# The output of the selective scan: three chunks of tokens in rotation instead of two

## The chip, the cores and the metric

The kernel runs on one core of a Trainium2 chip. The metric is the time of one execution on the device in microseconds (us), lower is better. Three runs of the kernel before the change took 13265.99, 13266.81 and 13270.98 us; the median is 13266.81. A profiled execution is a separate run, with its own time.

A core has several engines that work side by side, each through its own instructions in order: TensorE (PE, matrix products; PEld is its loading of weights), VectorE (DVE), ScalarE (ACT) and GpSimd (POOL). SyncE (SP) issues data transfers. They wait for one another through semaphores. SBUF is the on-chip memory with 128 partitions, PSUM the memory with eight banks into which PE writes.

## The reference, cut to what matters

The network takes four images of 56 x 56 positions with 128 channels. Each image passes four layers, each of the form x = x + layer(group_norm(x)): window attention, a selective state-space scan (mamba), a deformable convolution, and window attention again. The change touches only the end of the second layer, behind the scan:

```python
# y: sum of the four scan directions, 256 channels; z: second half of group_norm(x) @ w_in
mu = jnp.mean(y, axis=-1, keepdims=True)
var = jnp.mean(jnp.square(y - mu), axis=-1, keepdims=True)
y = (y - mu) * jax.lax.rsqrt(var + LN_EPS) * ln_w + ln_b
y = y * jax.nn.silu(z)
return y @ w_out
...
x = x + _L1_conv_ref(_gn(x), ...)
```

So each position needs a layer norm over 256 channels, a gate silu(z), a product with w_out (256 to 128 channels) and a residual addition. Channels lie on the partitions, in two halves of 128, so the mean and the variance over channels are matrix products.

## The kernel before

`run` (L1368) works through the images one after the other: `swin("L0")`, `mamba`, `deform`, `swin("L3")`. `mamba` calls `mamba_conv`, `mamba_scan` and `mamba_out` in turn; the change is in `mamba_out` (L1139 to L1198), which runs once per image, four times in all. The result of the scan lies in `ya` (two halves, 3136 positions), the residual stream in `x`.

`mamba_out` cuts the 3136 positions of an image into NCK = 7 chunks of CH = 448. The pool is opened under `manual_schedule()`: the instructions of each engine stay in the order in which the program writes them, so the order of the calls is the schedule. All its PSUM tiles share one tag with eight banks, taken in rotation. These are the steps for a chunk c:

- `mean`: PE multiplies `ya` by a matrix that yields minus the mean (`pm`, two products, L1149). DVE adds `pm` to each half of `ya` and gets the centred `xc` (L1153); ACT squares both halves into `sq` (L1155).
- `gate`: DVE normalizes the chunk of `x` with the group norm's mean and deviation into `xg` (`gn_apply`, L137). For each half, PE multiplies by `w_in` (`pz`, L1163) and ACT applies Silu into `z` (L1164).
- `spread`: PE sums the squares (`ln_pv`, L156, eight small products), ACT takes the square root (L158), DVE the reciprocal (L159), giving `ln_rs`, with positions on the partitions.
- `scale`: PE turns `ln_rs` and spreads it over all partitions (`ln_pb`, L1173, four products); DVE multiplies each half of `xc` by it (L1175), ACT applies `ln_w` and `ln_b` (Identity with scale and bias, L1177), DVE multiplies by `z` (L1178).
- `out`: PE multiplies `xc` by `w_out` (`pmo`, L1184), DVE adds the result to `x` (L1185) and takes the statistics for the next group norm (`stats`, L115).

An fp32 product appears in the profile as more than one matmul record: `pm`, `pz` of both halves and `pmo` have four each, `ln_pb` eight, `ln_pv` sixteen. ACT needs a table load (ACT_TABLE_LOAD) when it goes from Silu to Sqrt or back.

The order of the calls is a loop over the chunks at L1188 to L1198: `spread(c)`, `mean(c+1)`, `gate(c+1)`, `out(c-1)`, `scale(c)`. Behind the stage, `deform` (L1213) starts with a memset of `gp` on POOL (L1229) and with a group norm that needs the statistics of all seven chunks.

Of the kernel before, what the change touches and what calls it, by code (L numbers as in the profile page):

```python
# [10 lines left out]
F32 = mybir.dt.float32  # L11
# [8 lines left out]
P = 128  # L20
HW = 56
L = HW * HW
CH = 448
NCK = L // CH
# [54 lines left out]
class _Net:  # L79
# [1057 lines left out]
            assert not plan and not soon  # L1137

    def mamba_out(self, x, ya, gn):  # L1139
        nc, tc, w = self.nc, self.tc, self.w["L1"]  # L1140
        with tc.tile_pool(name="mo", bufs=2) as sb, tc.tile_pool(name="mo_ps", bufs=8, space=PSUM) as ps, tc.manual_schedule():
            bank = lambda name: ps.tile([P, 512], F32, tag="mm", name=name)
            part = lambda c: slice(c * CH, (c + 1) * CH)
            m = {}

            def mean(c):
                pm = bank("pm")
                for j in range(2):
                    nc.tensor.matmul(pm[:, :CH], lhsT=self.center[2][1], rhs=ya[:, j, part(c)], start=(j == 0), stop=(j == 1))  # L1149
                xc = m["xc", c] = sb.tile([P, 2, CH], F32, tag="xc", name="xc", bufs=3)  # L1150
                sq = m["sq", c] = sb.tile([P, 2, CH], F32, tag="sq", name="sq")
                for j in range(2):
                    nc.vector.tensor_add(xc[:, j, :], pm[:, :CH], ya[:, j, part(c)])  # L1153
                for j in range(2):
                    nc.scalar.activation(sq[:, j, :], xc[:, j, :], AF.Square)  # L1155

            def gate(c):
                xg = sb.tile([P, CH], F32, tag="xg", name="xg2")
                self.gn_apply(xg, x[:, part(c)], gn)
                z = m["z", c] = sb.tile([P, 2, CH], F32, tag="z", name="z", bufs=3)  # L1160
                for j in range(2):
                    pz = bank("pz")
                    nc.tensor.matmul(pz[:, :CH], lhsT=w["w_in"][:, (2 + j) * P : (3 + j) * P], rhs=xg, start=True, stop=True)  # L1163
                    nc.scalar.activation(z[:, j, :], pz[:, :CH], AF.Silu)  # L1164

            def spread(c):
                m["rs", c] = self.ln_spread(m.pop(("sq", c)), bank, sb)

            def scale(c):
                xc, rs = m["xc", c], m.pop(("rs", c))  # L1170
                pb = bank("ln_pb")
                for i in range(CH // QB):
                    nc.tensor.matmul(pb[:, i * QB : (i + 1) * QB], lhsT=rs[:, i : i + 1].to_broadcast([QB, P]), rhs=self.ident[:QB, :QB], start=True, stop=True)  # L1173
                for j in range(2):
                    nc.vector.tensor_mul(xc[:, j, :], pb[:, :CH], xc[:, j, :])  # L1175
                for j in range(2):
                    nc.scalar.activation(xc[:, j, :], xc[:, j, :], AF.Identity, bias=w["ln_b"][:, j : j + 1], scale=w["ln_w"][:, j : j + 1])  # L1177
                nc.vector.tensor_mul(xc, xc, m.pop(("z", c)))  # L1178

            def out(c):  # L1180
                xc = m.pop(("xc", c))
                po = bank("pmo")
                for j in range(2):
                    nc.tensor.matmul(po[:, :CH], lhsT=w["w_out"][:, j * P : (j + 1) * P], rhs=xc[:, j, :], start=(j == 0), stop=(j == 1))  # L1184
                nc.vector.tensor_add(x[:, part(c)], x[:, part(c)], po[:, :CH])  # L1185
                self.stats(x, c)

            mean(0)  # L1188
            gate(0)
            for c in range(NCK):  # L1190
                spread(c)
                if c + 1 < NCK:
                    mean(c + 1)
                    gate(c + 1)
                if c >= 1:
                    out(c - 1)
                scale(c)
            out(NCK - 1)  # L1198


    def deform_prepare(self):
# [269 lines left out]
```

## Time and profile before

| what | value |
|---|---|
| median of three runs | 13266.81 us |
| the profiled execution | 13274.82 us |
| its span, first to last instruction | 13273.0 us |
| PE busy | 11709.4 us (88%) |
| POOL busy | 9942.5 us (75%) |
| DVE busy | 9579.6 us (72%) |
| ACT busy | 7564.2 us (57%) |
| mean granted PE clock | 0.933 of full |
| group L1153, DVE, two additions per chunk | 56 x, median 615 ns |
| group L1155, ACT, two squares per chunk | 56 x, median 576 ns |
| group L1164, ACT, two Silu per chunk | 56 x, median 543 ns |
| group L1164, ACT, table load | 28 x, 1283 ns |
| group L1175, DVE, two products per chunk | 56 x, median 614 ns |
| group L1177, ACT, two scalings per chunk | 56 x, median 754 ns |
| group L1178, DVE, product with z | 28 x, median 1093 ns |
| group L1185, DVE, addition to x | 28 x, median 622 ns |

28 is seven chunks in four images. The profile gives each instruction's start and length. In a timeline, neighbouring instructions of one kind are merged into a row with their count; a bracket at the end gives how long the engine stood idle before the row and which instruction, by engine, tile and line, ended the wait. "issue" there means that the profile shows nothing that it waited for. Two instructions of one engine can overlap a little[...]. The ends of matmuls are modelled. The granted clock is the share of PE's full speed that it was allowed.

### The profile page before, as it was taken

The numbers are of one execution on the slowest core, as the hardware profiler recorded it, in microseconds if no ns is written. First come the engines' busy times: TensorE is split into PE (matmuls) and PEld (weight loads), VectorE is DVE, ScalarE is ACT, GpSimd is POOL, SyncE is SP. The second block draws the span as 40 slices with busy tenths as digits, with TensorE's granted clock in tenths as the row PEclk, the third lists the DMA queues.
The fourth block names the chain that finished last, engine by engine and source line by source line (L and its number), as shares of the span: only waits on it lengthen the run. The fifth ranks groups of instructions, "written<-read, shape, count | busy, mean of one in ns | idle before, by whom it ended". The sixth has DMA issues, their size and how long they took to land. (4 is left out here: it accounts for less than half of the span.)

```text
span 13273.0 us, 218239 instructions
## 1 busy us (share of the span) xinstructions
PE 11709.4 (88%) x85716; PEld 7457.0 (56%) x85716; DVE 9579.6 (72%) x11831; ACT 7564.2 (57%) x19130; POOL 9942.5 (75%) x6852
## 2 busy tenths in 40 slices
PE   8999995799999999579999899956998989995799
PEld 4448883444544888344454488834445448883444
DVE  6649996665564999666566599966646649996664
ACT  5567772356556777235655677723565567772356
POOL 4949994488494999448849499944975949994497
PEclk9999997799999999779999999977999999997799
DMA  2000004200000000420000000042000000004200
GB/s 100 1 14 4 5 4 116 79 1 7 5 1 14 4 5 4 115 80 1 7 5 1 14 4 5 4 118 77 1 8 4 1 14 5 5 4 123 71 1 6
DMA packets 181178, 344.60 MB, mean 26 GB/s; under 512 B 20104, under 2 KB 101416, under 8 KB 180024
## 3 DMA queue, kind: packets, MB, share of 16 engines
q0 software_dynamic: 80640, 231.28, 6.2%
q1 hardware_dynamic: 99224, 97.83, 2.3%
q8 instruction: 678, 11.11, 0.3%
q14 instruction: 348, 2.85, 0.1%
q10 hardware_dynamic: 288, 1.53, 0.0%
HBM read 256.04 MB, written 74.52 MB: 25 GB/s over the span
## 5 line engine op out<-in xcount | busy, mean ns | idle before, releaser
L555 POOL TENSOR_TENSOR es<-es,e 128x896 f32<-128x896 f32 x2016 | 4159.6, 2088 | 132.6 <-ACT e L549 74.7
L350 DVE TENSOR_REDUCE mx<-pm 128x1 f32<-128x512 f32 (+1 forms) x4928 | 3059.2, 672 | 1404.8 <-PE pm L349 790.7
L549 ACT ACTIVATE e<-pst 128x448 f32<-128x448 f32 (+1 forms) x5600 | 2677.8, 544 | 1893.5 <-PE pst L547 1349.3
L1066 DVE TENSOR_TENSOR_SCAN hs<-da,dbu 128x928 f32<-128x928 f32 x1792 | 3633.5, 2071 | 54.3 <-ACT dbu L1059 29.0
L1075 POOL TENSOR_TENSOR hs<-hs,cb 128x896 f32<-128x896 f32 x1792 | 3484.2, 1961 | 26.9 <-ACT carry L1070 21.9
L349 PE MATMUL pm<-ks,qs 32*128 32x512 f32 (+1 forms) x9856 | 2912.8, 636 | 13.3 <-DVE nm L371 7.8
L547 PE MATMUL pst<-qs,ks 32*128 32x448 f32 x11200 | 2685.8, 548 | 0.0
L1084 PE MATMUL yt<-w_C,hs 128*116 128x128 f32 x14336 | 1866.1, 273 | 1.1 <-POOL hs L1075 1.1
L542 PE MATMUL pst<-nm,sel 32*128 32x448 f32 x5600 | 1639.2, 614 | 0.0
L1084 PEld LDWEIGHTS yt<-w_C,hs 128*116 128x116 f32 x14336 | 1570.8, 135 | 2.1 <-POOL hs L1075 2.1
L1048 PE MATMUL dbu<-dgb,ut 112*128 112x224 f32 x7168 | 1258.4, 298 | 268.9 <-DVE hs L1066 268.8
L571 PE MATMUL po<-e,va 128*32 128x448 f32 (+1 forms) x11200 | 1352.4, 551 | 0.1
L349 PEld LDWEIGHTS pm<-ks,qs 32*128 32x128 f32 x9856 | 925.9, 186 | 744.0 <-DVE mx L350 617.8
L1308 POOL DMA_INDIRECT g<-tab,idx x1008 | 940.3, 933 | 453.5 <-issue 429.7
L1048 PEld LDWEIGHTS dbu<-dgb,ut 112*128 112x128 f32 x7168 | 945.4, 192 | 534.4 <-DVE hs L1066 524.4
L1002 ACT ACTIVATE da<-dl,A 128x112 f32<-128x112 f32 x3584 | 1194.5, 383 | 0.1
L547 PEld LDWEIGHTS pst<-qs,ks 32*128 32x128 f32 x11200 | 1098.7, 185 | 102.3 <-issue 13.7
L1334 PE MATMUL pvt<-w_C,g 112*128 112x112 f32 x2016 | 400.1, 365 | 735.6 <-issue 610.6
L542 PEld LDWEIGHTS pst<-nm,sel 32*128 32x128 f32 x5600 | 571.0, 184 | 739.9 <-DVE mx L350 387.1
L1335 ACT COPY vt<-pvt 128x336 f32<-128x336 f32 x336 | 147.2, 438 | 1190.6 <-PE pvt L1334 1186.1
L1334 PEld LDWEIGHTS pvt<-w_C,g 112*128 112x128 f32 x2016 | 312.7, 201 | 827.4 <-issue 791.1
L1070 ACT COPY carry<-hs 128x32 f32<-128x32 f32 x1792 | 397.8, 222 | 624.4 <-DVE hs L1066 616.1
(230 smaller groups left out, 15785.8 us busy)
## 6 DMA issues: line engine op xcount, KB each, us to landing
tab<-zero SPq DMA_DIRECT2D x4, 6728.0 KB
g<-tab,idx POOLq DMA_INDIRECT x1008, 3.4
tab<-gt SPq DMA_DIRECT2D x32, 448.0 KB
dl_d<-dl SPq DMA_DIRECT2D x28, 448.0 KB
dl<-dl_d SPq DMA_DIRECT2D x56, 224.0 KB
tab<-gt SPq DMA_DIRECT2D x32, 336.0 KB
out_dram<-x SPq DMA_DIRECT2D x28, 224.0 KB
x<-in_x_dram SPq DMA_DIRECT2D x21, 224.0 KB
```

Of the source, the lines that this page charges most:

```text
L349: nc.tensor.matmul(pm[:, :m], lhsT=qs[head(h), q.start : q.start + P], rhs=ks[head(h), keys], start=True, stop=True)
L350: nc.vector.tensor_reduce(mx[:, home[i][1], h, kc : kc + 1], pm[:, :m], AX.X, ALU.max)
L542: nc.tensor.matmul(t[:, :CH], lhsT=self.sel[head(h), :], rhs=nm[head(h), part(qc)], start=True, stop=False)
L547: nc.tensor.matmul(t[:, :CH], lhsT=ks[head(h), k * KB : (k + 1) * KB], rhs=qs[head(h), part(qc)], start=False, stop=True)
L549: nc.scalar.activation(e[:nk, j, :], t[:nk, :CH], AF.Exp, scale=SCALE)
L555: nc.gpsimd.tensor_tensor(s, es[g - 1, p][:nk] if k == 1 else s, e[:nk], ALU.add)
L571: nc.tensor.matmul(m["po"][head(h), :CH], lhsT=va[:nk, k, head(h)], rhs=src(h)[:nk], start=(k == 0), stop=(k == NKB - 1))
L1002: nc.scalar.activation(m["da"][:, :, n, 2:], dl(), AF.Exp, scale=A[:, j, n : n + 1])
L1048: nc.tensor.matmul(pu[:, 8 * h : 8 * h + 8, 2 + tb * TB : 2 + (tb + 1) * TB], lhsT=made[g]["ut", 2 * r + tb][:, d, :], rhs=made["r", g // ...
L1066: nc.vector.tensor_tensor_scan(flat(pairs[u // 2][:, d % 2]), flat(made[g]["da"][:, r]), flat(banks.pop(u)), 0.0, ALU.mult, ALU.add)
L1075: nc.gpsimd.tensor_tensor(hs, hs, made["r", g // 2]["cb"][:, :, r * HW : (r + 1) * HW], ALU.mult)
L1084: nc.tensor.matmul(sums[q][:YR, e * P : (e + 1) * P], lhsT=hs[:, n, :], rhs=self.ident, start=(n == 0), stop=(n == NST // 2 - 1), is_trans ...
```

## The change

The steps are cut finer and put into a new order. `mean` keeps only the product on PE; `less` takes the additions and squares. `tokens` takes the normalization out of `gate`. `gated` takes the product with z out of `scale`. `out` keeps only the product, and `store` takes the addition to `x` and the statistics. The loop runs over c from -1 to NCK and calls, where the chunk exists: `mean(c+1)`, `gated(c-1)`, `less(c+1)`, `scale(c)`, `gate(c+1)`, `out(c-1)`, `tokens(c+2)`, `spread(c+1)`, `store(c-1)`. So the chunks c-1, c and c+1 are at work in one round, and `xg` is made one round before its use. The tile `xc` has four buffers in place of three. The instructions themselves, their shapes and their number stay as they are.

```diff
--- before.py
+++ after.py
@@ -1137,6 +1137,8 @@
             assert not plan and not soon
 
     def mamba_out(self, x, ya, gn):
+
+
         nc, tc, w = self.nc, self.tc, self.w["L1"]
         with tc.tile_pool(name="mo", bufs=2) as sb, tc.tile_pool(name="mo_ps", bufs=8, space=PSUM) as ps, tc.manual_schedule():
             bank = lambda name: ps.tile([P, 512], F32, tag="mm", name=name)
@@ -1144,19 +1146,25 @@
             m = {}
 
             def mean(c):
-                pm = bank("pm")
+                pm = m["pm", c] = bank("pm")
                 for j in range(2):
                     nc.tensor.matmul(pm[:, :CH], lhsT=self.center[2][1], rhs=ya[:, j, part(c)], start=(j == 0), stop=(j == 1))
-                xc = m["xc", c] = sb.tile([P, 2, CH], F32, tag="xc", name="xc", bufs=3)
+
+            def less(c):
+                pm = m.pop(("pm", c))
+                xc = m["xc", c] = sb.tile([P, 2, CH], F32, tag="xc", name="xc", bufs=4)
                 sq = m["sq", c] = sb.tile([P, 2, CH], F32, tag="sq", name="sq")
                 for j in range(2):
                     nc.vector.tensor_add(xc[:, j, :], pm[:, :CH], ya[:, j, part(c)])
                 for j in range(2):
                     nc.scalar.activation(sq[:, j, :], xc[:, j, :], AF.Square)
 
+            def tokens(c):
+                m["xg", c] = sb.tile([P, CH], F32, tag="xg", name="xg2")
+                self.gn_apply(m["xg", c], x[:, part(c)], gn)
+
             def gate(c):
-                xg = sb.tile([P, CH], F32, tag="xg", name="xg2")
-                self.gn_apply(xg, x[:, part(c)], gn)
+                xg = m.pop(("xg", c))
                 z = m["z", c] = sb.tile([P, 2, CH], F32, tag="z", name="z", bufs=3)
                 for j in range(2):
                     pz = bank("pz")
@@ -1175,27 +1183,36 @@
                     nc.vector.tensor_mul(xc[:, j, :], pb[:, :CH], xc[:, j, :])
                 for j in range(2):
                     nc.scalar.activation(xc[:, j, :], xc[:, j, :], AF.Identity, bias=w["ln_b"][:, j : j + 1], scale=w["ln_w"][:, j : j + 1])
+
+            def gated(c):
+                xc = m["xc", c]
                 nc.vector.tensor_mul(xc, xc, m.pop(("z", c)))
 
             def out(c):
                 xc = m.pop(("xc", c))
-                po = bank("pmo")
+                po = m["po", c] = bank("pmo")
                 for j in range(2):
                     nc.tensor.matmul(po[:, :CH], lhsT=w["w_out"][:, j * P : (j + 1) * P], rhs=xc[:, j, :], start=(j == 0), stop=(j == 1))
-                nc.vector.tensor_add(x[:, part(c)], x[:, part(c)], po[:, :CH])
+
+            def store(c):
+                nc.vector.tensor_add(x[:, part(c)], x[:, part(c)], m.pop(("po", c))[:, :CH])
                 self.stats(x, c)
 
-            mean(0)
-            gate(0)
-            for c in range(NCK):
-                spread(c)
-                if c + 1 < NCK:
-                    mean(c + 1)
-                    gate(c + 1)
-                if c >= 1:
-                    out(c - 1)
-                scale(c)
-            out(NCK - 1)
+            def do(f, c):
+                if 0 <= c < NCK:
+                    f(c)
+
+            tokens(0)
+            for c in range(-1, NCK + 1):
+                do(mean, c + 1)
+                do(gated, c - 1)
+                do(less, c + 1)
+                do(scale, c)
+                do(gate, c + 1)
+                do(out, c - 1)
+                do(tokens, c + 2)
+                do(spread, c + 1)
+                do(store, c - 1)
 
 
     def deform_prepare(self):
```

## The prediction

> **What bounds the kernel now.** The page's own tables don't show this stage: its groups are too small for the costliest list and its lines are not in the chain of waits. I therefore asked the tiles that the change touches for their times, then the busy time of the stage in each of the four images. It runs from the first `pm` matmul behind the scan to the end of the last `stats` on `x`; columns are window, length, then busy time (count) of PE, weight loads, DVE, ACT, POOL, then the granted PE clock and the DMA share.
>
> ```profile
> core 0: us, PE busy (x) PEld busy (x) DVE busy (x) ACT busy (x) POOL busy (x), PEclk, DMA share, GB/s
> 2029.18:2110.27 81.09, 57.54 (x252) 35.49 (x252) 35.70 (x63) 44.21 (x63) 1.26 (x1) 0.92 0.00 1
> 5347.31:5429.53 82.22, 58.37 (x252) 35.38 (x252) 35.59 (x63) 44.31 (x63) 1.26 (x1) 0.88 0.00 0
> 8661.98:8745.21 83.23, 59.67 (x252) 36.12 (x252) 35.70 (x63) 44.32 (x63) 1.26 (x1) 0.86 0.00 0
> 11969.03:12052.10 83.07, 59.35 (x252) 36.16 (x252) 35.72 (x64) 44.31 (x63) 1.26 (x1) 0.86 0.00 1
> ```
>
> The stage takes 329.6 us of 13273.0 (2.5%). Nothing else runs beside it (POOL 1.26, no DMA), and no engine is full: PE 71%, ACT 54%, DVE 43%. The next stage starts from its last `stats`, so a microsecond saved here is one off the end. The limit must be a loop of waits between engines; the timeline of one round without a slow clock (2062.08 to 2072.01, 9.93 us: PE 7.21 busy, ACT 6.27, DVE 5.04) shows it, engine by engine. First DVE, then ACT, then PE:
>
> ```profile
> 2062.28 0.62 DVE L1185 TENSOR_TENSOR x<-x,pmo 128x448 f32<-128x448 f32 x1 [3.43 <-PE pmo L1184]
> 2062.94 0.63 DVE L115 BATCH_NORM_STATS2 gn_st<-x 128x6 f32<-128x448 f32 x1
> 2063.48 1.14 DVE L1175 TENSOR_TENSOR xc<-ln_pb,xc 128x448 f32<-128x448 f32 x2
> 2065.57 1.09 DVE L1178 TENSOR_TENSOR xc<-xc,z 128x896 f32<-128x896 f32 x1 [0.95 <-ACT xc L1177]
> 2067.14 0.18 DVE L159 RECIPROCAL ln_rs<-ln_rs 112x4 f32<-112x4 f32 x1 [0.48 <-ACT ln_rs L158]
> 2067.24 1.13 DVE L1153 TENSOR_TENSOR xc<-pm,ya 128x448 f32<-128x448 f32 x2
> 2068.28 0.51 DVE L137 TENSOR_SCALAR xg<-x,gn_mean,gn_rstd 128x448 f32<-128x448 f32 x1
> ```
> ```profile
> 2064.12 1.41 ACT L1177 ACTIVATE xc<-xc,w_L 128x448 f32<-128x448 f32 x2 [2.79 <-DVE xc L1175]
> 2065.55 1.28 ACT L158 ACT_TABLE_LOAD   x1
> 2066.85 0.26 ACT L158 ACTIVATE ln_rs<-ln_pv,eps 112x4 f32<-112x4 f32 x1
> 2067.93 1.04 ACT L1155 ACTIVATE sq<-xc 128x448 f32<-128x448 f32 x2 [0.82 <-DVE xc L1153]
> 2068.99 1.28 ACT L1164 ACT_TABLE_LOAD   x1
> 2070.29 0.98 ACT L1164 ACTIVATE z<-pz 128x448 f32<-128x448 f32 x2
> ```
> ```profile
> 2068.93 1.74 PE L1163 MATMUL pz<-xg,w_L 128*128 128x448 f32 x4 [2.72 <-DVE xg L137]
> 2070.51 1.67 PE L1184 MATMUL pmo<-xc,w_L 128*128 128x448 f32 x4
> 2072.01 1.04 PE L1173 MATMUL ln_pb<-w_C,ln_rs 112*128 112x112 f32 x8
> 2072.89 1.65 PE L156 MATMUL ln_pv<-w_C,sq 128*112 128x1 f32 x16
> 2074.40 1.75 PE L1149 MATMUL pm<-ya,w_C 128*128 128x448 f32 x4
> 2078.86 3.18 PE L1163 MATMUL pz<-xg,w_L 128*128 128x448 f32 x4 [2.71 <-DVE xg L137]
> ```
>
> The reader is to see one ring. DVE's store (2062.28), stats and two products feed ACT's scaling (2064.12); behind that stand the table load and the square root (2066.85); the reciprocal, two additions and `xg` follow on DVE; `xg` frees PE's `pz` (2068.93), and `pmo` follows, for which the next store waits (3.43 us). In the ring PE stands idle 2.7 us a round. The last PE row is the same `pz` at a slow clock, 3.18 for 1.74; such rounds took 11.3 to 11.4 us instead of 9.93, so the slow clock lies on the path. From the throttle-free pieces I put a stage together: first `pm` to first `ln_pb` 11.7 (image 1), next round 11.27 less 1.5, four rounds of 9.93, last round 6.2, drain about 8: 75.4. The four stages have a mean of 82.4, so the slow clock costs about 7.0 each.
>
> **What the Trainium skill says.** Perfetto Trace Analysis, Per-engine timelines: ACT and DVE are strict FIFO; the trace agrees, every row above is in program order. ScalarE: Activation LUTs, What ACT_TABLE_LOAD costs: 1283 ns and a drain of 1380 ns. The trace agrees on the first (1283 in every one), not on the second: sqrt starts 0.02 after its load, and the load 0.02 after the scaling. I use 1.285. Same page, Table sets: cheap functions such as identity are in every set; the trace shows Identity (L1271) behind the group norm's Sqrt, and Square (L1155) behind L158, without a load. TensorE: Matmul & The Clock Gate, Part 1: a PE idle for about 3.4 us falls to half clock. Here 2.7 us sufficed now and then, and 3.4 us always (the last `pmo` took 3.3 in all four images).
>
> **The change part by part.** No instruction is added or removed; `xc` gets a fourth buffer. The order per round becomes: PE `pm`(c+1), `ln_pb`(c), `pz`(c+1), `pmo`(c-1), `ln_pv`(c+1); DVE product with z (c-1), two additions (c+1), two products (c), `xg`(c+2), reciprocal (c+1), store and stats (c-1); ACT two squares (c+1), two scalings (c), load, two Silu (c+1), load, sqrt (c+1). Table loads stay two a round, since Silu and Sqrt still alternate.
>
> *Waits that go.* `pz` finds `xg` made a round ago, `pmo` its product, the store its `pmo`. *Wait that is late next.* The reciprocal stands on DVE ahead of store, stats, product with z and additions, although none of them needs it; ACT reaches its sqrt only behind both loads, and its next squares wait for these additions. So a new ring of ACT and DVE. Lags from the rows above (start to start): sqrt to reciprocal 0.29, reciprocal 0.10, store 0.65, stats 0.54, product with z 1.0 (1.09 less the overlap of neighbours), addition to square 0.66, squares 1.07, scalings 1.40, load 1.285, Silu 0.98, load 1.285: 9.26 us a round. `ln_pb` and the products on it end 0.1 us before ACT asks for them. PE needs 6.9 of 9.26 and waits 2.36 at `ln_pb`, for the reciprocal.
>
> *PE's slack.* A half clock adds at most about 1.5 us to a round's PE work, as above. `ln_pb` has 1.0 us before DVE comes to it (and loses 0.9), `pz` 3.3, `pmo` over 5, `ln_pv` 2.4, `pm` 3. So I cost the slow clock at nothing in the middle; if the cover were gone, it is 1.5 in each such round, as today.
>
> *Buffers.* Six banks a round of eight: each bank is reused by an instruction whose predecessor in it was read a round earlier. `sq`, `xg`, `ln_rs` with two, `z` with three, `xc` with four also find theirs free. Cost nothing. The memset of `gp` on POOL behind the stage still has the group norm's 6.5 us as cover.
>
> *The sum for one stage.* First `pm` to first sqrt: 1.72 + 0.66 + 1.07 + 1.285 + 0.98 + 1.285 = 7.0. To the second: 7.25 (no store, no product with z; the scaling waits for `ln_pb`). To the third: 9.26 less store and stats = 8.07. Four full rounds: 37.04. Drain behind the last sqrt: 0.29 + 0.10 + 1.19 + 1.24 to `pmo`(5), 1.71 to its store, 1.19, product with z 1.24, `pmo`(6) 1.71, store and stats 1.3: 9.97. Sum 69.3. Laid out in the same way the old order gives 74.1 against 75.4 above, so the way is short by about 1.2: 70.5. Slow clock: the first `pm` in three of four images, +0.8 each, so 0.6 in the mean; both `pmo` in the drain, +1.5 each (waits of 1.4 and 2.6 us on PE behind one of 3.9). 74.1 per stage against 82.4: 8.3 saved, times 4 is 33 us. The profiled execution took 13274.8 (span 13273.0 and 1.8 around it), 8 above the median of 13266.8; so 13241 for such an execution and 13233 for the median.
>
> **Bounds.** No slow clock at all and no shortfall: 69.3, saves 52. As much slow clock as today (7.0 on 70.5): saves 4.9 a stage, 20. What a measurement of this kernel can tell from no change is about 0.2%, 26.5 us.
>
> **Rivals.**
> 1. *The new ring is hardly shorter* and slow clock remains: 9.26 against 9.93 is only 0.67 a round; if PE's waits at `ln_pb` bring as many slow windows and these reach DVE (`ln_pb` has just 0.1 us to spare at half clock), 20 us: 13247. For it: the 2.36 us of idle PE in every round. Against: everything but `ln_pb` has over 2 us of slack.
> 2. *PE becomes the bound* at about 7.3 a round, if ACT and DVE overlapped better than in my order: 5 rounds shorter by 2 more, 4 times: 40 more, 13193. Against: ACT alone has 6.27 a round, and between sqrt and squares it stands idle 3 us.
> 3. *Slower: PE stays at half clock through whole rounds.* Then its 6.9 is 13.8, above the ring. Fully cold stages: 7 x 4 x (13.8 - 9.3) = 126 on top of -33, 13360. From 27% of cold rounds on the change loses. For it: PE is now idle once in every round. Against: the gap is shorter than today's 2.7, which left most rounds fast.
> 4. *Slower: further table loads*, if Identity behind Sqrt called for one and Silu for another: 2 x 1.285 x 28 = 72, 13306. Against: L1271.
>
> **How the numbers follow.** Forecast (saving over 26.5, around 33) 0.74; rival 1 0.14; rival 2 0.04; rivals 3 and 4 0.08. Faster 0.78, same 0.14, slower 0.08. Range from the bounds, reaching a little past both: 13212 to 13254.
>
> **What shows each step.** Right: a middle round of 9.2 to 9.5 us in all images, slow clock or not; DVE's longest wait at the reciprocal for ACT's sqrt (4 us a round), PE's at `ln_pb` for the reciprocal, ACT's at the squares (3 us); no wait for `xg` or at the store but in the drain; 14 loads a stage; stages of 72 to 76. Wrong: rounds over 9.9 or under 9, waits at `pm` or `pz` for banks, a third load, or stretches at half clock through whole rounds.

## The result and the profile after

The changed kernel takes 13235.55 us in the median of 10 runs (13223.56 to 13245.72); the kernel before, on the same chips, 13269.67 (13261.48 to 13305.55). The ratio, worked out from the single runs and so not the quotient of the two medians (0.9974), is 0.997 with a 95% interval of 0.9961 to 0.998; the medians lie 34 us apart. The span of the profiled execution went from 13273.0 to 13243.9 us.

The view of busy time, for the same four stages of the changed kernel (first `pm` to last `stats`; columns as before):

```profile
core 0: us, PE busy (x) PEld busy (x) DVE busy (x) ACT busy (x) POOL busy (x), PEclk, DMA share, GB/s
2028.28:2101.94 73.66, 57.89 (x252) 35.47 (x252) 33.90 (x62) 43.70 (x63) 1.25 (x1) 0.88 0.00 1
5336.18:5409.35 73.17, 57.70 (x252) 35.77 (x252) 34.00 (x62) 43.70 (x63) 1.26 (x1) 0.88 0.00 1
8637.29:8711.75 74.46, 58.96 (x252) 36.41 (x252) 34.01 (x62) 43.70 (x63) 1.26 (x1) 0.87 0.00 1
11940.63:12014.34 73.71, 59.57 (x252) 36.28 (x252) 33.91 (x62) 43.70 (x63) 1.25 (x1) 0.86 0.00 1
```

The engines do the same work as before, in 295.0 us instead of 329.6: 8.6 less per stage. The granted clock is no higher (0.86 to 0.88 against 0.86 to 0.92). DVE in a middle round (its timeline, first image):

```profile
2070.54 0.18 DVE L159 RECIPROCAL ln_rs<-ln_rs 112x4 f32<-112x4 f32 x1 [4.39 <-ACT ln_rs L158]
2070.63 0.59 DVE L1198 TENSOR_TENSOR x<-x,pmo 128x448 f32<-128x448 f32 x1
2071.26 0.63 DVE L115 BATCH_NORM_STATS2 gn_st<-x 128x6 f32<-128x448 f32 x1
2071.80 1.07 DVE L1189 TENSOR_TENSOR xc<-xc,z 128x896 f32<-128x896 f32 x1
2072.79 1.15 DVE L1158 TENSOR_TENSOR xc<-pm,ya 128x448 f32<-128x448 f32 x2
2073.86 1.14 DVE L1183 TENSOR_TENSOR xc<-ln_pb,xc 128x448 f32<-128x448 f32 x2
2074.92 0.50 DVE L137 TENSOR_SCALAR xg<-x,gn_mean,gn_rstd 128x448 f32<-128x448 f32 x1
2079.82 0.18 DVE L159 RECIPROCAL ln_rs<-ln_rs 112x4 f32<-112x4 f32 x1 [4.40 <-ACT ln_rs L158]
```

And ACT in the same round:

```profile
2073.50 1.05 ACT L1160 ACTIVATE sq<-xc 128x448 f32<-128x448 f32 x2 [3.00 <-DVE xc L1158]
2074.50 1.42 ACT L1185 ACTIVATE xc<-xc,w_L 128x448 f32<-128x448 f32 x2
2075.94 1.28 ACT L1172 ACT_TABLE_LOAD   x1
2077.23 0.98 ACT L1172 ACTIVATE z<-pz 128x448 f32<-128x448 f32 x2
2078.23 1.28 ACT L158 ACT_TABLE_LOAD   x1
2079.52 0.26 ACT L158 ACTIVATE ln_rs<-ln_pv,eps 112x4 f32<-112x4 f32 x1
```

DVE's waits of before, for `pmo`, for the scaling and for the square root, have become a single one of 4.4 us at the reciprocal. Once it is released, DVE works without a break through store, statistics, product with z and the additions, and ACT's squares wait 3.0 us for the first of these additions. From one reciprocal to the next: 9.28 us.

PE in the third image, from the `ln_pb` of one middle round to that of the next, with a slow clock in it:

```profile
8671.30 1.93 PE L1181 MATMUL ln_pb<-w_C,ln_rs 112*128 112x112 f32 x8 [1.96 <-DVE ln_rs L159]
8673.02 2.61 PE L1171 MATMUL pz<-xg,w_L 128*128 128x448 f32 x4
...
8680.57 1.15 PE L1181 MATMUL ln_pb<-w_C,ln_rs 112*128 112x112 f32 x8 [0.36 <-DVE ln_rs L159]
```

`ln_pb` and `pz` take 1.93 and 2.61 where 1.15 and 1.68 are usual. PE's wait at the next `ln_pb` shrinks from about 2.0 to 0.36, and the round is 9.27, as without a slow clock. One or two such rounds come in each stage, and none is made longer by it for good: in the second image a slow round takes 8.79 where the others have 8.19, and the next 8.59 where they have 9.19. The last round (up to the last `ln_pb`) takes 9.37 in all four images, in two of them with slow instructions and in two without.

In the drain of the first image both `pmo` take twice their time with nothing beside them:

```profile
2091.58 3.33 PE L1195 MATMUL pmo<-xc,w_L 128*128 128x448 f32 x4 [1.04 <-DVE xc L1189]
2097.27 3.35 PE L1195 MATMUL pmo<-xc,w_L 128*128 128x448 f32 x4 [2.37 <-DVE xc L1189]
```

For the stages of all runs I took the same marks: the wait of PE ahead of the first `pm` (lead), first `pm` to first `ln_pb`, middle rounds from `ln_pb` to `ln_pb` (the first ones and the last of the six in a stage are left out), and the last `ln_pb` to the end (drain), in us:

| run | lead | to first ln_pb | middle round | drain | stage, mean |
|---|---|---|---|---|---|
| before | 1.54 | 11.70 to 14.10 | 9.93 or 11.38 | 9.37 to 9.91 | 82.4 |
| changed | 2.13 | 8.45 to 9.24 | 9.28 | 11.65 to 12.53 | 73.8 |
| store ahead of spread | 2.13 | 8.44 to 9.26 | 8.10 | 10.36 to 12.10 | 67.6 |
| product with z in its own round | 2.13 | 8.46 to 9.28 | 8.28 | 7.70 to 8.64 | 65.0 |
| xg in the round of its use | 1.54 | 8.26 to 10.67 | 10.03, or 11.5 to 13.0 | 10.58 to 12.53 | 85.8 |
| before, PE's waits filled | 1.54 | 11.70 to 12.81 | 9.87 | 7.79 | 75.7 |
| store and product ahead | 2.13 | 8.42 to 9.19 | 7.45 | 9.51 to 12.11 | 63.8 |
| no table loads | 2.13 | 7.87 | 6.99 | 12.46 to 12.53 | 60.0 |
| changed, drain filled | 2.13 | 8.46 to 9.28 | 9.28 | 8.83 to 9.51 | 71.1 |
| both ahead, xg(0) late, drain filled | 1.54 | 8.26 to 10.67 | 7.38 | 8.15 | 62.8 |
| both ahead, head and drain filled | 4.39 to 5.10 | 7.93 to 8.64 | 7.38 | 8.15 | 60.8 |

### The profile page after: what moved, and what is told of

Same layout as the page of the kernel before. It is cut to its first block, busy times and chain, and to the rows that moved or that the text cites. A ratio compares the mean times of both kernels' runs of the same rounds, so it can differ in the third digit from the quotient of the medians.

```text
span 13243.9 us, 218251 instructions
## 1 busy us (share of the span) xinstructions
PE 11713.7 (88%) x85716; PEld 7459.5 (56%) x85716; DVE 9575.5 (72%) x11831; ACT 7563.6 (57%) x19130; POOL 9941.6 (75%) x6852
```

## The experiments

The rest of the kernel, outside the stages, varied between single profiled executions by some 30 us (span less stages: 12943.6 before, 12948.9 changed, 12953.2 changed with the drain filled, 12920.6 without table loads, all on chips with about the same time before). So the mechanism is read from the stages, and the times are given as ratios to the kernel before on the same chip. Where the interval of a ratio overlaps that of the change (0.9961 to 0.998), the times don't tell the run from the changed kernel; the stages do. The first four runs were on a chip where the kernel before takes 13493.84 us; the others on one with 13272.24, the last with 13267.84.

The question was which ring sets the round after the change, and which of its parts earn anything.

### What stands behind the reciprocal: the store

```diff
-                do(spread, c + 1)
                 do(store, c - 1)
+                do(spread, c + 1)
```

> The changed kernel with store(c-1) called ahead of spread(c+1), so that DVE does the store and the statistics before the reciprocal instead of behind it. Theory of the DVE/ACT ring: store and statistics (1.19 us) leave the ring and fall into DVE's wait; a middle round goes from 9.28 to 8.08, a stage from 73.8 to about 67.8, the kernel is about 24 us faster than the changed one, about 58 us faster than the one before. Rival (PE sets the round: its slow clock and its waits for xg were the gain, DVE's order behind the reciprocal costs nothing): round stays at 9.28, no difference to the changed kernel.

Measured: rounds of 8.10 in all four images, stages of 67.6, 13442.32 us, ratio 0.9952 (0.9936 to 0.9969), which just overlaps that of the change. Two waits of DVE in one of these rounds:

```profile
2065.75 0.62 DVE L1198 TENSOR_TENSOR x<-x,pmo 128x448 f32<-128x448 f32 x1 [0.80 <-PE pmo L1195]
2069.35 0.18 DVE L159 RECIPROCAL ln_rs<-ln_rs 112x4 f32<-112x4 f32 x1 [2.32 <-ACT ln_rs L158]
```

DVE now waits 0.80 for `pmo` and only 2.32 at the reciprocal; ACT's squares wait 1.82 instead of 3.00. The two instructions cost about 1.2 us a round (9.28 to 8.10) by their place alone. The rival falls.

### One part undone: the product with z back in its own round

```diff
-                do(gated, c - 1)
                 do(less, c + 1)
                 do(scale, c)
+                do(gated, c)
                 do(gate, c + 1)
```

> The changed kernel with one part undone: the product with z stands directly behind the scaling of its own chunk again (gated(c) behind scale(c)), so it waits for ACT in the same round. Theory of the DVE/ACT ring: putting that product into another round costs, since it stands on the ring; undone, 0.98 us leave the ring, a middle round is 8.3 instead of 9.28, a stage about 67 to 68, the kernel 22 to 26 us faster than the changed one. Rival (each step in another round than the one it waits for is what saves): DVE waits about 1 us for the scaling in each round, a round is 0.5 to 1 us longer, 10.0, and the kernel 15 to 25 us slower than the changed one.

Measured: rounds of 8.28, stages of 65.0, 13418.23 us, ratio 0.9934 (0.9917 to 0.995). DVE in one of these rounds:

```profile
2061.36 0.18 DVE L159 RECIPROCAL ln_rs<-ln_rs 112x4 f32<-112x4 f32 x1 [2.35 <-ACT ln_rs L158]
2061.45 0.59 DVE L1198 TENSOR_TENSOR x<-x,pmo 128x448 f32<-128x448 f32 x1
2062.07 0.63 DVE L115 BATCH_NORM_STATS2 gn_st<-x 128x6 f32<-128x448 f32 x1
2062.62 1.14 DVE L1158 TENSOR_TENSOR xc<-pm,ya 128x448 f32<-128x448 f32 x2
2063.67 1.15 DVE L1183 TENSOR_TENSOR xc<-ln_pb,xc 128x448 f32<-128x448 f32 x2
2065.76 1.09 DVE L1189 TENSOR_TENSOR xc<-xc,z 128x896 f32<-128x896 f32 x1 [0.95 <-ACT xc L1185]
...
2069.63 0.18 DVE L159 RECIPROCAL ln_rs<-ln_rs 112x4 f32<-112x4 f32 x1 [2.35 <-ACT ln_rs L158]
```

The product now waits 0.95 us for the scaling of its own round, the very wait that the change took away, and the round is 1.0 shorter. That wait lies in time in which DVE would wait for the square root anyway; without it the product stands behind the reciprocal, where ACT waits for DVE. This part of the change costs. The drain gets 4 us shorter too, so that a stage is 65.0 where 67 to 68 were expected: in the changed kernel the last product with z (2096.14 in image 1) stands behind a store that waits 2.44 for `pmo`, and here it stands ahead of it.

### Another part undone: xg in the round of its use

```diff
-            tokens(0)
...
+                do(tokens, c + 1)
                 do(gate, c + 1)
                 do(out, c - 1)
-                do(tokens, c + 2)
```

> The changed kernel with another part undone: xg is made in the round of its use again, behind the two products of scale (tokens(c+1) ahead of gate(c+1)). Theory of rings: PE's pz, pmo and ln_pv then hang on xg, and this chain (products 1.06, xg 0.65, pz 1.5, pmo 1.5, ln_pv 1.7) is 0.75 us longer than ACT's way from the products to its sqrt, so a middle round is 10.0 instead of 9.28, a stage 77.5 to 80 (with the slow clock on the path again), the kernel 16 to 26 us slower than the changed one. Rival (xg is covered by PE's slack of over 3 us): round stays at 9.28, the head 0.6 us shorter, the kernel 0 to 3 us faster.

Measured: rounds of 10.03 where the clock is full, and one or two of 11.5 to 13.0 in each stage; stages of 85.8, 13497.48 us, ratio 0.9999 (0.999 to 1.0007). So with `xg` in this place the whole gain is gone, and the stage is longer than the 82.4 of before: the rest of the new order gains nothing with `xg` there. The place is not quite that of before, where `xg` stood ahead of the two products of `scale`; here it stands behind them. How long a round would be with `xg` between the additions and the products was not run. The ring is as expected, the slow clock costs more than I had allowed for. PE of this run, and after it ACT, in the same stretch:

```profile
2070.96 1.77 PE L1171 MATMUL pz<-xg,w_L 128*128 128x448 f32 x4 [2.78 <-DVE xg L137]
...
2080.99 3.35 PE L1171 MATMUL pz<-xg,w_L 128*128 128x448 f32 x4 [2.78 <-DVE xg L137]
2084.14 3.03 PE L1195 MATMUL pmo<-xc,w_L 128*128 128x448 f32 x4
```
```profile
2073.71 1.28 ACT L158 ACT_TABLE_LOAD   x1
2075.75 0.26 ACT L158 ACTIVATE ln_rs<-ln_pv,eps 112x4 f32<-112x4 f32 x1 [0.76 <-PE ln_pv L156]
```

The square root, which in the changed kernel starts right behind its load, now waits 0.76 for `ln_pv`: PE is on the ring again, by the 0.75 reckoned. And since it is, each half-clock `pz` and `pmo` (3.35 and 3.03 for 1.77 and 1.67) goes straight into the round.

### What the slow clock cost before

```diff
+            def fill(n):
+                for i in range(n):
+                    nc.tensor.matmul(warm[:, :CH], lhsT=self.center[2][1], rhs=ya[:, 0, part(0)], start=True, stop=True)
...
                     mean(c + 1)
+                    fill(3 if c >= 1 else 2)
                     gate(c + 1)
```

(and `fill` in the head and the drain, with `warm` in a bank of its own)

> The kernel before, with additional products on PE whose result nobody reads, in the waits for xg and in the drain, and one PSUM bank less for the others: it measures what the slow clock cost there. Theory: with no waits on PE over 1 us the slow clock goes, all middle rounds take 9.93, a stage 75.5 to 77 instead of 82.4, the kernel 22 to 28 us faster than before. Rival (the slow clock isn't caused by these waits, or costs nothing on the path): some rounds still take 11.3, a stage 82 or more, no gain or slower since pz queues behind the added products.

Measured: 9.87 in every middle round, stages of 74.9 to 76.0, 13470.82 us, ratio 0.9975 (0.9965 to 0.9986). PE in such a round:

```profile
2064.40 2.42 PE L1192 MATMUL warm<-ya,w_C 128*128 128x448 f32 x6
2067.18 1.77 PE L1163 MATMUL pz<-xg,w_L 128*128 128x448 f32 x4 [0.37 <-DVE xg L137]
```

`pz` waits for the same `xg`, but PE has been at work meanwhile, and no `pz` in the middle rounds is slow any more. In the kernel before, the waits brought the slow clock, and it cost 82.4 - 75.7, about 6.6 us a stage, head and drain included.

### Both edits together

```diff
-                do(gated, c - 1)
...
                 do(tokens, c + 2)
-                do(spread, c + 1)
                 do(store, c - 1)
+                do(gated, c)
+                do(spread, c + 1)
```

> The changed kernel with the edits of the two runs before it together: store(c-1) and then gated(c) ahead of spread(c+1), so that DVE has nothing but the reciprocal and the two additions between ACT's sqrt and ACT's next squares. Theory of the DVE/ACT ring: the ring is sqrt to reciprocal 0.29, reciprocal 0.10, addition to square 0.69, squares and scalings with a small gap 2.7, both loads and Silu 3.55, so a middle round is 7.35 (PE then needs 7.0 of it), a stage 61 to 64, the kernel 40 to 48 us faster than the changed one, ratio to before about 0.994. Rival (PE at 7.0 with its slow clock is the bound below 8.3): rounds of 8.3 to 9, no gain over the better of the two single edits.

(The two edits are that of the store and that of the product with z; the product stands behind the store here.)

Measured: rounds of 7.45, stages of 63.8, 13201.42 us, ratio 0.9942 (0.9925 to 0.9959). DVE:

```profile
2060.01 0.18 DVE L159 RECIPROCAL ln_rs<-ln_rs 112x4 f32<-112x4 f32 x1 [0.67 <-ACT ln_rs L158]
2060.15 1.15 DVE L1158 TENSOR_TENSOR xc<-pm,ya 128x448 f32<-128x448 f32 x2
2061.48 1.16 DVE L1183 TENSOR_TENSOR xc<-ln_pb,xc 128x448 f32<-128x448 f32 x2 [0.18 <-PE ln_pb L1181]
2062.55 0.50 DVE L137 TENSOR_SCALAR xg<-x,gn_mean,gn_rstd 128x448 f32<-128x448 f32 x1
2064.50 0.62 DVE L1198 TENSOR_TENSOR x<-x,pmo 128x448 f32<-128x448 f32 x1 [1.45 <-PE pmo L1195]
```

The wait at the reciprocal is down from 4.39 to 0.67; ACT's for DVE from 3.00 to 0.89. The store waits 1.45 for `pmo` again, in time in which DVE would otherwise wait for the square root: 0.67 of that wait is still left at the reciprocal.

### Without table loads

```diff
-                    nc.scalar.activation(z[:, j, :], pz[:, :CH], AF.Silu)
+                    nc.scalar.activation(z[:, j, :], pz[:, :CH], AF.Square)
```

> The changed kernel with Silu replaced by Square, so that ACT has the same number of activations and no table load (the gate is computed wrong by that, as left out part). Theory of the DVE/ACT ring: both loads (2.57 us) leave the ring, it would be 6.7, below what PE needs, so PE sets the round at 7.0; a stage 56 to 60. Rival (the loads lie in ACT's wait for DVE and cost nothing, as its 3 us of idle time a round suggest): round stays at 9.28.

Measured: one load a stage instead of 14, rounds of 6.99, stages of 60.0, 13169.98 us, ratio 0.992 (0.9901 to 0.994). Here PE has no wait inside the round, and the square root waits for it:

```profile
2051.63 0.26 ACT L158 ACTIVATE ln_rs<-ln_pv,eps 112x4 f32<-112x4 f32 x1 [0.46 <-PE ln_pv L156]
```

The two loads, 2.57 us, lie on the ring; with them gone PE sets the round at its own work, so the round gets 2.29 shorter and not 2.57. So rival 2 of the prediction, PE as the bound, exists, but behind the ring.

### The slow clock in the drain

```diff
+                if c == NCK - 1:
+                    fill(4)
                 do(scale, c)
                 do(gate, c + 1)
+                if c >= NCK - 1:
+                    fill(1 if c == NCK - 1 else 3)
                 do(out, c - 1)
```

> The changed kernel with additional products on PE, whose result nobody reads, in the waits of the last two rounds, and one PSUM bank less for the others: it measures what the slow clock costs in the drain. Theory: both pmo of the drain take 1.7 instead of 3.3, the drain goes from 12.5 to about 9.4, a stage from 73.8 to about 70.5; the middle rounds stay at 9.28. Rival (the slow clock there has another cause than the waits): pmo still takes 3.3, stage 73 to 74.

Measured: drain 9.51 in three images and 8.83 in one (there a slow clock and the added products make the last round 10.27), stages of 71.1, middle rounds still 9.28; 13231.49 us, ratio 0.9967 (0.9953 to 0.998). All `pmo` of the drain take 1.67 to 1.74. The slow ones cost 73.8 - 71.1 = 2.7 us a stage. The times don't tell this run from the changed kernel.

### Two tries at the head

The first on top of "both edits": `xg` of chunk 0 made behind the first `pm`, and the drain filled.

```diff
-            tokens(0)
...
+                if c < 0:
+                    tokens(0)
                 do(gate, c + 1)
```

> The run with store and gated ahead of spread, and in addition xg of the first chunk made behind the first pm, and additional products in PE's waits of the drain. Theory: lead of the stage 0.6 us shorter (1.54 as in the kernel before), drain about 7.8, rounds 7.35, stage 60 to 61.5, the kernel 50 to 56 us faster than the changed one, ratio to before about 0.9935. Rival (the head and the drain are covered by the neighbouring stages): same time as without these two edits.

Measured: 13175.63 us, ratio 0.9929 (0.9913 to 0.9946), stages of 62.8, less gain than expected in them. The lead is 0.6 shorter, but in three images the way to the first `ln_pb` is 10.65 to 10.67, 2.4 longer than in the fourth (8.26), where the first `pm` and `pz` have the full clock. PE in one of the three:

```profile
5307.07 2.30 PE L1151 MATMUL pm<-ya,w_C 128*128 128x448 f32 x4 [1.54 <-DVE ya L1105]
5311.19 3.36 PE L1171 MATMUL pz<-xg,w_L 128*128 128x448 f32 x4 [1.82 <-DVE xg L137]
```

`pz` waits 1.82 for `xg`, stays slow, and the first square root hangs on it. Of the kernels that leave nothing out this one has the fastest median; but only 1.7 us a stage of lead and stage together (65.96 to 64.30), 7 us, of the 26 between it and the run before comes from the stages. The other 19 lie outside, within the spread named above, and I can't assign them.

The second went back to the early `xg`, filled the drain in the same way, and added `fill(2)`, reading `x`, ahead of the first `pm`.

> As the run with store and gated ahead of spread (xg of the first chunk made ahead of the first pm, as in the changed kernel), with additional products on PE in the drain and two in PE's wait ahead of the first pm. Theory: the late first xg of the run before was what cost that run 2.4 us in the head of three images (first pm to first ln_pb 10.7 there); here that stretch is 7.5 to 8.3 in all images, rounds 7.45, drain 8.2, a stage 60 to 61.5, lead 2.1, the kernel 48 to 54 us faster than the changed one. Rival (a slow clock in the head comes whatever xg and the waits do): first pm to first ln_pb 9 to 10.7, stage 62 to 63.5.

Measured: first `pm` to first `ln_pb` 7.93 to 8.64, rounds 7.38, stages of 60.8, but a lead of 4.39 to 5.10: the filler, which doesn't read `ya`, itself waited 2.13 for the scan's last additions to `ya` and pushed `pm` back. Why it waited (perhaps for its bank) is not shown. 13197.73 us, ratio 0.9941 (0.9923 to 0.9958). That the early `xg` avoids the slow head of the run before is borne out, also by "both edits", which has no fillers (8.42 to 9.19); the filler ahead of `pm` bought nothing (lead and stage 65.7).

## Why the prediction was right

- *The time.* 13233 was forecast, 13235.55 measured; for the profiled execution a saving of 33 was worked out, and lead and stage together give (83.9 - 75.9) x 4 = 32. That the medians agree to 3 us is partly luck: the part outside the stages varies by some 30 us, and the two profiled executions lie 29.1 apart, since it was 5.3 longer in the second.
- *The new ring.* Laid out at 9.26, measured 9.28; the waits stand where they were put (reciprocal 4.4, squares 3.0, `ln_pb` 2.0 where 2.36 was put). Moving its members out, one at a time and together, gave 8.10, 8.28 and 7.45 where 8.08, 8.3 and 7.35 were reckoned. This is shown.
- *The slow clock.* "I cost the slow clock at nothing in the middle": shown in the round at 8671, where slow `ln_pb` and `pz` took 1.7 more and the round stayed at 9.27. The term of 7.0 per stage before measured 6.6 by filling the waits. In the drain 3.0 was put down, and filling it took out 2.7.
- *Where the 8.6 us per stage come from.* With PE's waits filled in both kernels they stand at 75.7 and 71.1. So about 4.6 are the shorter way through the stage, and 4.0 are slow clock that no longer lies on the path. That division is a reckoning from two runs, whose fillers aren't the same.
- *Table loads.* Two a round, as forecast, no drain behind them; rival 4 fell.
- *Rival 1* (20 us): slow windows did come, one or two a stage, and at 8671 one fell on `ln_pb`, but they didn't reach DVE: its 0.1 us of slack was enough. *Rival 3* did not occur: the slow spells ended within a round.

Three terms were off and largely cancelled. The head was laid at 7.0 to the first square root, 7.5 to `ln_pb`, with 0.6 for the slow clock; it took 8.45 to 9.24, so 1.2 over the 7.5 on average, and the first `pm` was slow in all four images and not in three. The allowance of 1.2 by which the method was taken to fall short wasn't needed: the middle rounds were right to 0.02. And the lead, which the prediction does not have, got longer: `tokens(0)` is called before the first `mean`, and its instruction came to stand among the scan's last additions to `ya`, for which `pm` waits. DVE at the start of the stage in the changed kernel:

```profile
2026.19 0.27 DVE L1105 TENSOR_TENSOR ya<-ya,pyb 128x112 f32<-128x112 f32 x1 [3.89 <-PE pyb L1100]
2026.66 0.51 DVE L137 TENSOR_SCALAR xg<-x,gn_mean,gn_rstd 128x448 f32<-128x448 f32 x1 [0.20 <-issue]
2027.09 1.05 DVE L1105 TENSOR_TENSOR ya<-ya,pyb 128x112 f32<-128x112 f32 x3
```

It costs 0.6 us of lead in each stage (2.13 for 1.54), 2.4 in all; the two runs in which `xg` of chunk 0 is made later have 1.54 again.

## What to carry to other kernels

An in-order engine should have only its urgent work behind its longest wait: the change earned its time by making `xg` a round early, and gave back 1.8 us a round (9.28 against 7.45) by placing store and product with z behind the reciprocal, where they hold up the engine that this one waits for. "In another round than what it waits for" is therefore no aim by itself; a short wait inside a longer one is free, and an instruction moved out of it may land on the ring. Before reordering, write the ring down with the start-to-start lags of one clean round: it gave every full-clock round here to 0.1 us, and told which move would pay.

## What was not expected of the hardware

PE's slow clock came with waits under 3 us that recur: 2.7 to 2.8 us once a round of about 10 us brought one or two slow spells a stage (before, and with `xg` late), and about 2 us a round of 9.28 still brought one or two. Waits of 0.87 to 1.03 a round (rounds of 8.10 and 8.28) brought none in the middle rounds. Where the line lies between these was not measured. In the window 2080.34 to 2083.73 of the changed kernel PE was busy throughout at a granted clock of 0.50. Each spell added 1.4 us to a round of before, and up to 2.9 where `pz` and `pmo` both fell into it. A few matmuls that nobody reads, placed in the wait, removed it in the middle rounds, at no cost to the round (9.87 against 9.93).
